# Sandwich layer on one core: first feed-forward norm on ScalarE and GpSimd, background products in quarters with rest steps, block 0's halves stored once

## The chip, the cores and the metric

The kernel runs on one core of one Trainium2 chip. The core has five engines with a queue of instructions each: TensorE (PE, matrix products; PEld is its weight load), VectorE (DVE), ScalarE (ACT), GpSimd (POOL) and SyncE (SP, which here only issues DMAs). Each engine works through its queue in order and waits on semaphores for the others. DMAs are issued from the queues of SP, ACT and POOL and run beside the engines. Products land in PSUM, eight banks of 512 float32 values on each of 128 partitions. The metric is the device time of one execution in microseconds; lower is better.

## What is computed

One transformer layer in float32 on 4096 tokens of 256 features:

```
x = x + layernorm(attention(layernorm(x)))
x = x + layernorm(ffn(layernorm(x)))

attention: q, k, v = x @ w_attn + b_attn, 16 heads of 16 features
           softmax(causal(q @ k.T / 4)) @ v, then @ w_proj + b_proj
ffn(x):    h = silu(x @ w1 * s1) * (x @ w2 * s2)        256 -> 1024
           h = gelu(h @ h1 * sh1); h = gelu(h @ h2 * sh2)  1024 -> 1024
           h @ w3 * s3                                  1024 -> 256
```

The feed-forward weights are drawn from -1, 0 and 1. The biases of attention are random.

## The kernel before, in words

The tokens are cut into 8 blocks of 512 (`NB`, `QB`), the 16 heads into 4 groups of 4 (`G`). An *item* (j, g) is query block j with head group g; there are 32 items, in order. Item (j, g) goes over the keys of blocks 0 to j in *steps* (`steps`, L876): 4j + 3 of them, with one or two units each, 8j + 5 *units* for the item and 1056 in all. A unit (`SharedUnit`, L828) is 1024 columns of scores for two heads in two PSUM banks: TensorE makes them (L843), VectorE takes their maximum (`mx`, L852), ScalarE the exponentials (`e_s`, L859), GpSimd clears what lies past the diagonal (L866), and three units later TensorE multiplies them with the values (`av`, L930). Three such pairs of banks go round (`ps_s`); one bank holds the `av` sums and one single bank (`ps_m`) is for everything else.

The score products take q and k in a rounded type (float32r). To keep the precision, q and k are split into a rounded upper half and the rest (`hi`, `lo`, in `features`, L519), and both halves are stored to DRAM twice, so that the 64 rows of a head's contraction hold all four pairs of halves. `load_rows` (L554) reads 128 such rows, two heads, in one DMA of 256 KB; `queries` (L566) and `keys` (L577) call it. The keys of the next item are asked for during the current one (`ask`, L585), for every item anew. All these loads go through SyncE's queue.

The rest of attention's work is *background*: generators that stop at marks and are run piece by piece between the steps. `prep(j)` (L599) loads block j, normalises it, transposes it (two groups of four 128x128 transposes), makes the k and q features (four products of two matmuls with 512 columns) and v. For blocks 0 and 1 its statistics and halves are VectorE's, later ScalarE's and GpSimd's. `project(j)` (L273) takes a finished block's weighed values through `w_proj`, its layer norm and the residual, and stores the sum in DRAM as `x1[j]`. Marks say what the next piece is: `PE` starts a product, `HALF` continues one, `ACT` is a pass of ScalarE, `BESIDE` is no stop here, `True` is anything else. A product and its continuation use the single bank `ps_m`, so an open product (`Background.open`) is finished before another begins.

After each step `Background.even(every)` (L95) runs at most one product piece, each `every` steps, and at most one ScalarE piece, likewise; other pieces run as they come. `every` is 1 for blocks 0 and 1, 2 for blocks 2 and 3, 3 from block 4 on (L1177). A piece is half a product: `prep` has 14 of them (two transposes, eight halves of features, four of v), `project` has 4. `finish` and the loop at L1138 run what is still missing when it is needed: q and k of block j + 1 at the start of item (j, 3), the whole prep at the start of block j.

Before the loop (L1115 to L1132) the kernel runs block 0's and block 1's norms, `biases` (L1102, which scales the q bias and makes the projection's share of the v bias, `pb`, from `wp`), block 0's features up to the first q, the loads of items 0 and 1, and the rest of block 0. Block 1's remaining prep then is background.

In the background also run `halve_weights` (L981, rounding the feed-forward weights on GpSimd) and, from item (7, 2) on, `norm_block(0, ...)` (L356) with `first_features` (L1060): the layer norm of `x1[0]` for the feed-forward, with statistics, scaling and lower halves on VectorE, and its eight transposes in one of the three score bank pairs. The result `xT0` is what the feed-forward begins with. `feed_forward` (L1249) then goes block by block through the four matrices on TensorE, and does the next block's norm (`norm_block` again) and the last block's `project` beside it.

Two flags computed on the device choose slower code for unusual data (`attention(False)`, `feed_forward(False, ...)`); they do not run here.

Of the kernel before, what the change touches and what calls it, by code (L numbers as in the profile page):

```python
# [17 lines left out]
P = 128  # L18
# [11 lines left out]
class Background:  # L30
# [6 lines left out]
    def __init__(self, beside=lambda: None):  # L37
        self.work = deque()
        self.beside = beside
        self.at = 0  # L40
        self.open = None

# [52 lines left out]
    def even(self, every):  # L95


        self.at += 1
        pe, act = not self.at % every, not (self.at + 1) % every
        for job in list(self.work):  # L100
            if job[3] in (self.PE, self.HALF):
                if pe and self.open in (None, job):
                    pe = False
                    self.run(job)
                    self.open = job if job[3] == self.HALF else None
            elif job[3] != self.ACT:
                self.run(job)
            elif act:
                act = False
                self.run(job)  # L110
# [7 lines left out]
def sandwich_kernel(  # L118
# [154 lines left out]
    def project(j, room):  # L273
# [35 lines left out]
        for half in range(0, NT, 2):  # L309
            ps = room.bank(f"py_{j}_{half}").rearrange("p (t f) -> p t f", t=2)  # L310
            for t in range(2):
                yield room.within(t)
                for c in range(DC):
                    nc.tensor.matmul(  # L314
                        ps[:, t, :],
                        lhsT=oT[:, c, (half + t) * P : (half + t + 1) * P],
                        rhs=wp[:, c, :],
                        start=(c == 0),
                        stop=(c == DC - 1),
                    )  # L320
# [83 lines left out]
    def attention(shared):  # L404
# [8 lines left out]
        with ExitStack() as actx:  # L413
# [22 lines left out]
            class Room:  # L436


                def within(self, n):
                    return Background.HALF if shared and n else Background.BESIDE  # L440
# [34 lines left out]
            def constants():  # L475
# [38 lines left out]
                (s, j): scratch.tile([H, 2, 2, HD, QB], F32, tag=f"{s}_{j}", name=f"{s}_{j}")  # L514
# [4 lines left out]
            def features(j, s, c, engine):  # L519
# [3 lines left out]
                for d in range(DC):  # L523
                    yield room.within(d)
                    nc.tensor.matmul(  # L525
                        ps,
                        lhsT=wqk[d][:, i * D + c * P : i * D + (c + 1) * P],
                        rhs=xTs[j][:, d, :],
# [16 lines left out]
                for half, part in enumerate((hi, lo)):  # L545
                    for d in range(2):
                        at = (d, half) if i else (half, d)
                        queue = nc.gpsimd if shared and j < 2 and half else nc.sync
                        queue.dma_start(
                            out=halves_of[s, j][8 * c : 8 * (c + 1), at[0], at[1]], in_=part  # L550
                        )
                stored.add((s, j, c))

            def load_rows(tag, name, key, j, h):  # L554

                t = (piece if key == "k" else query)(tag, name, F32R)
                nc.sync.dma_start(
                    out=t.bitcast(F32),
                    in_=halves_of[key, j][h : h + 2].rearrange("h a b d n -> (h a b d) n"),
                )  # L560
# [16 lines left out]
            def keys(n, c):  # L577

                for pr in range(2):
                    kT[n, c, pr] = load_rows(  # L580
                        f"k{asked[0] % RING}_{pr}", f"k{n}_{c}_{pr}", "k", c, 4 * (n % G) + 2 * pr
# [17 lines left out]
            def prep(j, engine=nc.gpsimd):  # L599
# [30 lines left out]
                for c in range(DC):  # L630
                    ps = room.bank(f"pt_{j}_{c}")
                    for t in range(NT):
                        nc.tensor.transpose(
# [11 lines left out]
                for half in range(0, NT, 2):  # L645
                    ps = room.bank(f"pv_{j}_{half}").rearrange("p (t f) -> p t f", t=2)
                    for t in range(2):
                        yield room.within(t)
                        for c in range(DC):
                            nc.tensor.matmul(  # L650
# [408 lines left out]

            def first_features(pts):  # L1060
# [41 lines left out]
            def biases():  # L1102
                nc.vector.tensor_scalar(bqk[:, 0:DC], bqk[:, 0:DC], SCALE, None, ALU.mult)
# [15 lines left out]
            biases()  # L1119
            while ("q", 0, 0) not in stored:  # L1120
                bg.piece(works[0])
            for n in range(2):
                queries(*items[n])
                keys(*chunks[n])
            while bg.piece(works[0]) is not False:
                pass
            if shared:
                bg.add(("prep", 1), works[1], PREP)
                bg.work[0][3] = Background.PE
            else:  # L1130
# [3 lines left out]
            for n, (j, g) in enumerate(items) if shared else ():  # L1134
# [14 lines left out]
                if (j, g) == (NB - 1, G - 2):  # L1149
                    for _ in halving:  # L1150
                        pass
                    bg.add(("norm", 0), norm_block(0, room, first_features), NORM)
# [3 lines left out]
                for p, (shapes, parts) in enumerate(steps(j)):  # L1156
# [19 lines left out]
                    if j < 2 or p < NT * j:  # L1176
                        bg.even(1 + j // 2 - j // 6)  # L1177
# [71 lines left out]
    def feed_forward(halves, xT0, W):  # L1249
# [6 lines left out]
        with ExitStack() as fctx:  # L1256
# [12 lines left out]
            class Room:  # L1269
                def within(self, n):  # L1270
                    return Background.BESIDE
# [236 lines left out]
```

## Time and profile before

| | |
|---|---|
| median of 3 runs | 2053.32 us (2049.6 to 2054.11) |
| the profiled execution's own time | 2048.42 us |
| its span, first to last instruction | 2046.5 us |
| mean granted TensorE clock | 0.986 |
| PE, DVE, ACT, POOL busy | 1825.3, 1609.8, 1399.2, 552.2 us |
| first score maximum | 39.8 us |
| blocks 0 to 3 of attention | 53.0, 75.1, 107.0, 147.8 us |
| blocks 4 to 7 | 185.7, 216.7, 253.8, 295.4 us |
| feed-forward | from 1378 us to the end |
| DMA | 202.09 MB, mean 99 GB/s |

Blocks are counted from their first score maximum to the next block's. A view by stretches gives, for each engine, how long it was busy and with how many instructions, and the clock that the throttle granted TensorE as a share of full speed. In a timeline a line is a group of equal instructions of one engine: its start, its duration, and in brackets how long the engine was idle before it and whose work ended that. "SPq" and "POOLq" are DMA issues. A wait is put down to what came last.

### The profile page before, as it was taken

The page shows a single profiled execution, that of the slowest core. Times are in us where ns is not written, and L with a number is a line of the kernel's source. Part 1 is how long each engine was busy: PE and PEld are TensorE (multiplying, and loading weights), DVE is VectorE, ACT ScalarE, POOL GpSimd, SP SyncE. Part 2 cuts the span into 40 slices and gives each one's busy share as a digit, 9 for nine tenths or more (in the row PEclk, how much of TensorE's full clock was granted, in tenths as well). Part 3 has the DMA queues.
Part 4 walks back from the last instruction along what each step waited for, and adds up shares of the span by engine and source line. Part 5 has one row for each costly group of instructions (what it writes and reads, how often), then busy time and mean ns, then how long its engine had stood idle before and what let it go on. Part 6 is the DMA issues. An engine that isn't in the chain of part 4 may idle for free.

```text
span 2046.5 us, 28401 instructions
## 1 busy us (share of the span) xinstructions
PE 1825.3 (89%) x10518; PEld 932.5 (46%) x10518; DVE 1609.8 (79%) x1894; ACT 1399.2 (68%) x1598; POOL 552.2 (27%) x871
## 2 busy tenths in 40 slices
PE   4799989988888888888888887889999999999997
PEld 2333332322322322223222222228888888888886
DVE  3689998998999999999999999985546456465453
ACT  2699999999999999999999998982212222222221
POOL 3264545434435335333333110000120000000000
PEclk8899999999999999999999998999999999999999
DMA  6756645444235333553234213103100000000000
GB/s 168 229 179 219 191 133 180 147 154 159 98 131 183 116 103 124 161 163 115 76 136 156 98 44 101 63 9 114 53 11 21 15 7 21 1 21 21 1 11 15
DMA packets 134909, 202.09 MB, mean 99 GB/s; under 512 B 16064, under 2 KB 60736, under 8 KB 134752
## 3 DMA queue, kind: packets, MB, share of 16 engines
q1 hardware_dynamic: 130496, 194.56, 29.3%
q0 software_dynamic: 2480, 4.35, 1.0%
q8 instruction: 87, 1.43, 0.3%
q10 hardware_dynamic: 1776, 1.18, 0.3%
q14 instruction: 70, 0.57, 0.1%
HBM read 137.91 MB, written 62.13 MB: 98 GB/s over the span
## 4 chain that ended last, share of the span: by engine, by line
PE 46%; ACT 21%; DVE 19%; issue 6%; DMA 4%; POOL 2%; SPq 1%; ACTq 0%; POOLq 0%; DVEq 0%
PE z L1358 21%; ACT e_s L859 19%; DVE mx L852 18%; PE av L930 7%; PE s L843 7%; PE za L1358 3%; PE zb L1358 2%; PE pyf L1440 2%; DMA k<-k 1%; PE py L314 1%; PE pk L525 1%; PE pv L650 1%; PE pq L525 1%; ACT junk L211 1%; DMA q<-hiq 0%
## 5 line engine op out<-in xcount | busy, mean ns | idle before, releaser
L852 DVE TENSOR_REDUCE mx<-s 128x1 f32<-128x1024 f32 x1056 | 1219.8, 1217 | 72.1 <-PE s L843 66.6
L859 ACT ACTIVATE e_s<-s,shift 128x1024 f32<-128x1024 f32 x1056 | 1153.6, 1117 | 104.9 <-DVE mx L852 81.9
L843 PE MATMUL s<-q,k 64*128 64x512 f32 (+3 forms) x2304 | 517.7, 468 | 161.2 <-ACT e_s L859 144.7
L930 PE MATMUL av<-e_s,v 128*32 128x512 f32 (+2 forms) x4576 | 572.8, 575 | 7.9 <-POOL e_s L866 5.7
L843 PEld LDWEIGHTS s<-q,k 64*128 64x128 f32 x2304 | 208.9, 185 | 752.9 <-ACT e_s L859 652.2
L1425 ACT ACTIVATE fb<-z,sh 128x512 f32<-128x512 f32 x128 | 88.1, 689 | 364.8 <-PE z L1358 340.2
L1358 PE MATMUL z<-hb_0l,h 128*128 128x512 f32 x512 | 199.5, 390 | 0.0
L1358 PE MATMUL z<-hb_0h,h 128*128 128x512 f32 x512 | 199.5, 390 | 0.0
L866 POOL TENSOR_SCALAR_AFFINE_SELECT e_s<-e_s 128x256 f32<-128x256 f32 (+1 forms) x224 | 94.7, 440 | 337.4 <-ACT e_s L859 337.4
L233 POOL TENSOR_TENSOR rstd<-ve,neghalf 128x4 f32<-128x4 f32 (+1 forms) x22 | 20.8, 944 | 608.8 <-DVE ve L231 603.0
L930 PEld LDWEIGHTS av<-e_s,v 128*32 128x32 f32 x4576 | 97.2, 109 | 151.5 <-issue 116.1
L1325 DVE CAST hb_1h<-fb 128x512 fp32r<-128x512 f32 x64 | 27.4, 428 | 155.7 <-ACT fb L1425 155.7
L1402 ACT ACTIVATE sl<-za,s 128x512 f32<-128x512 f32 x64 | 44.0, 690 | 120.4 <-PE za L1358 60.9
L1325 DVE CAST hb_0h<-fb 128x512 fp32r<-128x512 f32 x64 | 28.1, 440 | 99.6 <-ACT fb L1425 99.6
L1358 PEld LDWEIGHTS z<-hb_0h,h 128*128 128x128 f32 x512 | 96.1, 188 | 20.0
L1358 PEld LDWEIGHTS z<-hb_0l,h 128*128 128x128 f32 x512 | 96.2, 188 | 19.8
L1011 POOL TENSOR_SCALAR wc<-wc 128x256 f32<-128x256 f32 x88 | 75.8, 861 | 7.8
L1010 POOL TENSOR_TENSOR wc<-wc,wh 128x256 f32<-128x256 f32 x88 | 64.3, 730 | 7.2
L1012 POOL TENSOR_TENSOR fit<-fit,wc 128x256 f32<-128x256 f32 x88 | 64.2, 730 | 7.3
L1009 POOL CAST wh<-wc 128x256 fp32r<-128x256 f32 x88 | 35.0, 397 | 108.4 <-DMA wc<-in_h_t_dram 75.9
L1440 PE MATMUL pyf<-w,hb_1l 128*128 128x256 f32 x256 | 61.8, 284 | 0.0
L1440 PE MATMUL pyf<-w,hb_1h 128*128 128x256 f32 x256 | 61.7, 283 | 0.0
(257 smaller groups left out, 1970.3 us busy)
## 6 DMA issues: line engine op xcount, KB each, us to landing
k<-k SPq DMA_DIRECT2D x288, 256.0 KB
q<-q SPq DMA_DIRECT2D x64, 256.0 KB
x<-in_x_dram SPq DMA_DIRECT2D x16, 512.0 KB
k<-hik SPq DMA_DIRECT2D x32, 256.0 KB
q<-hiq SPq DMA_DIRECT2D x32, 256.0 KB
wc<-in_h_t_dram SPq DMA_DIRECT2D x64, 128.0 KB
r_h<-wh SPq DMA_DIRECT2D x64, 128.0 KB
h<-r_h SPq DMA_DIRECT2D x32, 256.0 KB
```

Of the source, the lines that this page charges most:

```text
L843: nc.tensor.matmul(self.both[:, i, col : col + n], lhsT=kT[G * j + g, c, pr][r, tt * P : (tt + 1) * P], rhs=qT[j, g][pr][r, QB - n :], sta ...
L852: nc.vector.tensor_reduce(next(columns), self.both.rearrange("p a n -> p (a n)"), AX.X, ALU.max)
L859: nc.scalar.activation(e, self.both, AF.Exp, bias=shifts[j])
L866: nc.gpsimd.affine_select(out=here, in_=here, compare_op=ALU.is_ge, fill=0.0, base=0, pattern=[[0, here.shape[1]], [1, P]], channel_multip ...
L930: nc.tensor.matmul(self.av[h * HW : (h + 1) * HW, QB - n :], lhsT=vb[kt // NT][:, kt % NT, o : o + HW], rhs=of(es, h), start=(kt == 0 or k ...
L1010: nc.gpsimd.tensor_tensor(w, w, hi, ALU.subtract)
L1011: nc.gpsimd.tensor_scalar(w, w, 0.0, None, ALU.is_equal)
L1012: nc.gpsimd.tensor_tensor(fit, fit, w, ALU.mult)
L1325: nc.vector.tensor_copy(hi, full)
L1358: nc.tensor.matmul(ps, lhsT=w[c], rhs=single(part[:, c, :]), start=(c == 0 and i == 0), stop=(c == kc - 1 and i == parts - 1),)
L1425: nc.scalar.activation(h, z, AF.Gelu, scale=sc[:, oc : oc + 1])
L1440: nc.tensor.matmul(ps[:, 0:D], lhsT=single(part[:, c, t * P : (t + 1) * P]), rhs=(w3_r if halves else w3_sb)[:, c, :], start=(c == 0 and i ...
```

## The change

Five things, in the order of the diff:

1. `Background.even` gets the number of product pieces for a step, the period of product steps, the period of ScalarE pieces, and a number of rest steps: with `rest`, the step that ends a product starts no other piece of TensorE or ScalarE, and product pieces pause until `rest` steps later. Blocks 0 to 2 run two pieces per product step (each step; each second step for block 2) with no rest; blocks 3 to 7 run one piece each step and rest 3. The ScalarE periods are 1, 1, 2, 2, 3, 3, 3, 2 for blocks 0 to 7.
2. Products are cut into quarters: features by half their columns and by the two matmuls, v and `py` by single matmuls, transposes into two and two. `prep` has 28 pieces, `project` 8.
3. Block 0's halves of q and k are stored once; its loads read the rows twice (`broadcast_to`), for k in two DMAs of 64 rows. The other blocks' copies lie in another order. Item 0's keys are loaded from GpSimd's queue.
4. Before the loop, `pb` is made after block 0's prep, and block 1's prep is run up to its first k feature.
5. Block 0's feed-forward norm is `norm_first`: sums and squares on ScalarE, scaling and both halves on GpSimd, transposes through the single bank in quarters. `project(6)` is finished before it is added.

```diff
-    def even(self, every):
+    def even(self, products, every, acts, rest):
         self.at += 1
-        pe, act = not self.at % every, not (self.at + 1) % every
+        pe = 0 if self.at % every or self.at < self.rested else products
+        act = self.at % acts == 1 % acts
         for job in list(self.work):
             if job[3] in (self.PE, self.HALF):
-                if pe and self.open in (None, job):
-                    pe = False
+                while pe and job[3] in (self.PE, self.HALF) and self.open in (None, job):
+                    pe -= 1
                     self.run(job)
                     self.open = job if job[3] == self.HALF else None
+                    if rest and not self.open:
+                        pe, act, self.rested = 0, False, self.at + rest
...
-                for d in range(DC):
-                    yield room.within(d)
+                cuts = 2 if shared else 1
+                for n, (cut, d) in enumerate(product(range(cuts), range(DC))):
+                    yield room.within(n)
+                    at = slice(cut * QB // cuts, (cut + 1) * QB // cuts)
                     nc.tensor.matmul(
-                        ps,
+                        ps[:, at],
                         lhsT=wqk[d][:, i * D + c * P : i * D + (c + 1) * P],
-                        rhs=xTs[j][:, d, :],
+                        rhs=xTs[j][:, d, at],
...
+                    queue = nc.gpsimd if shared and j < 2 and half else nc.sync
+                    kept = halves_of[s, j][8 * c : 8 * (c + 1)]
+                    for d in range(2) if j else ():
                         at = (d, half) if i else (half, d)
-                        queue = nc.gpsimd if shared and j < 2 and half else nc.sync
+                        queue.dma_start(out=kept[:, at[0], :, at[1]], in_=part)
+                    if not j:
+                        queue.dma_start(out=kept[:, :, half] if i else kept[:, half], in_=part)
...
+                elif key == "k":
+                    for i in range(2):
+                        rows = part[i : i + 1].rearrange("u d b n -> u (d b) n")
+                        queue.dma_start(
+                            out=to[i * P // 2 : (i + 1) * P // 2],
+                            in_=rows.broadcast_to([2, 2 * HD, QB]),
+                        )
+                else:
+                    rows = part.rearrange("h a (d u) n -> (h a d) u n", u=1)
+                    queue.dma_start(out=to, in_=rows.broadcast_to([P // 2, 2, QB]))
...
+            def norm_first():
+                xj = xb[0] = load_block(0, x1[0])
+                for _ in range(3):
+                    yield True
+                yield Background.ACT
+                mv = stat.tile([P, NT, 2], F32, tag="mv", name="mvf_0")
+                for t in range(NT):
+                    mean_of(xj[:, t, :], mv, t)
+                    yield Background.ACT
+                    spread_of(xj[:, t, :], mv, t)
+                    yield Background.ACT if t < NT - 1 else True
+                rstd = rstd_of(mv)
+                xh = room.tokens(0)
+                for t in range(NT):
+                    shift_and_scale(xh[:, t, :], xj[:, t, :], mv, rstd, t, nc.gpsimd)
+                    yield True
+                yield True
+                yield Background.PE
...
+                for c in range(DC):
+                    ps = room.bank(f"ptf_0_{c}")
+                    for t in range(NT):
+                        if t == NT // 2:
+                            yield Background.HALF
+                        nc.tensor.transpose(
+                            ps[:, t * P : (t + 1) * P], xh[:, t, c * P : (c + 1) * P], ident
+                        )
+                    nc.scalar.copy(xT[:, c, :], ps)
+                    hi, lo = (t[:, c, :] for t in xT0)
+                    nc.gpsimd.tensor_copy(hi, xT[:, c, :])
+                    nc.gpsimd.tensor_tensor(lo, xT[:, c, :], hi, ALU.subtract)
+                    yield Background.PE if c < DC - 1 else True
...
-            biases()
+            nc.vector.tensor_scalar(bqk[:, 0:DC], bqk[:, 0:DC], SCALE, None, ALU.mult)
             while ("q", 0, 0) not in stored:
                 bg.piece(works[0])
             for n in range(2):
                 queries(*items[n])
-                keys(*chunks[n])
+                keys(*chunks[n], nc.sync if n or not shared else nc.gpsimd)
             while bg.piece(works[0]) is not False:
                 pass
+            biases()
             if shared:
                 bg.add(("prep", 1), works[1], PREP)
                 bg.work[0][3] = Background.PE
+                while ("k", 1, 0) not in stored:
+                    bg.step()
...
-                    bg.add(("norm", 0), norm_block(0, room, first_features), NORM)
+                    bg.finish(("project", NB - 2))
+                    bg.add(("norm", 0), norm_first(), NORM)
...
-                        bg.even(1 + j // 2 - j // 6)
+                        bg.even(1 + (j < 3), 1 + (j == 2), (1, 1, 2, 2, 3, 3, 3, 2)[j], 3 * (j > 2))
```

## The prediction

> **What bounds the kernel now.** I read the engines' busy time by stage first (columns: stretch; PE, PEld, DVE, ACT and POOL busy with counts; granted clock; DMA share; GB/s). The stretches are block 0's attention, blocks 1, 5, 6 and 7, and the feed-forward stage; their bounds are the first score maxima (`mx`) of each block.
>
> ```profile
> core 0: us, PE busy (x) PEld busy (x) DVE busy (x) ACT busy (x) POOL busy (x), PEclk, DMA share, GB/s
> 39.00:92.00 53.00, 40.18 (x212) 17.36 (x212) 29.00 (x33) 29.73 (x40) 16.95 (x38) 0.77 0.72 221
> 92.00:168.00 76.00, 68.64 (x446) 25.93 (x446) 63.58 (x61) 67.21 (x90) 37.47 (x65) 1.00 0.62 206
> ...
> 608.00:825.00 217.00, 186.65 (x1202) 58.28 (x1200) 209.60 (x188) 206.34 (x227) 92.28 (x146) 1.00 0.41 133
> 825.00:1079.00 254.00, 218.78 (x1404) 68.27 (x1402) 246.36 (x222) 241.06 (x243) 95.07 (x147) 1.00 0.41 131
> 1079.00:1378.00 299.00, 248.35 (x1584) 73.47 (x1584) 289.62 (x282) 276.57 (x270) 39.39 (x66) 0.98 0.24 79
> 1378.00:2046.00 668.00, 653.38 (x3144) 551.03 (x3144) 349.81 (x707) 159.53 (x222) 52.76 (x61) 0.99 0.08 24
> ```
>
> The feed-forward's 668 us are TensorE's, in an order the change leaves alone. In late attention VectorE (97%) and ScalarE (95%) are both nearly full: back to back one `mx` takes 1.13 us (42 in 47.63 us on the chain). Block 0 is another thing: no engine is full, the clock is 0.77 and DMA moves 221 GB/s. Next the ramp, in order of time.
>
> ```profile
> 9.42 1.38 DVE L237 TENSOR_SCALAR x<-x,mv,rstd 128x256 f32<-128x256 f32 x4 [1.00 <-POOL rstd L233]
> 12.37 2.05 PE L1106 MATMUL pb<-wp,bv 128*128 128x256 f32 x4 [12.37 <-DMA wp<-in_w_proj_dram]
> 14.21 1.06 PE L633 MATMUL pt<-ident,x 128*128 128x128 f32 x4
> ...
> 23.24 2.60 SPq L549 DMA_DIRECT2D q<-hiq  x2
> ...
> 33.79 0.84 SPq L557 DMA_DIRECT2D q<-q  x2
> ...
> 38.98 0.80 PE L843 MATMUL s<-q,k 64*128 64x512 f32 x2 [5.88 <-DMA k<-k]
> ```
>
> Block 0's rows are normalised at 10.8, but their transposes wait in TensorE's queue behind `pb`, which waits for `wp`. The q halves' stores are issued at 23.24 and landed at 33.8; the first scores wait for the loads. TensorE's own windows show the price of that wait (PE busy, clock, DMA):
>
> ```profile
> 33.00:36.00 3.00, 0.09 (x1) 1.00 0.74 206
> 36.00:39.00 3.00, 0.03 (x2) 0.57 0.96 318
> 39.00:42.00 3.00, 1.57 (x4) 0.50 0.99 305
> ```
>
> The granted clock is 0.50 from 36.4 to 53.5, for most of the first item. Then the block norm of block 0 (item (7, 2)), on VectorE:
>
> ```profile
> 1232.29 0.42 DVE L196 BATCH_NORM_STATS2 bn<-x 128x6 f32<-128x256 f32 x1
> ...
> 1244.83 1.38 DVE L237 TENSOR_SCALAR y<-x,mvf,rstd 128x256 f32<-128x256 f32 x4 [1.14 <-POOL rstd L233]
> ...
> 1250.18 0.69 DVE L1067 TENSOR_TENSOR xT0l<-ptf,xT0h 128x512 fp32r<-128x512 f32 x1 [1.72 <-ACT xT0h L1066]
> ```
>
> Last, what a background product does in mid-attention (a half product of `project`, and the maximum after it):
>
> ```profile
> 706.75 1.13 PE L314 MATMUL py<-wp,oo 128*128 128x256 f32 x4
> ...
> 708.36 1.22 DVE L852 TENSOR_REDUCE mx<-s 128x1 f32<-128x1024 f32 x1 [0.20 <-PE s L843]
> ```
>
> **The change, part by part.** The sum goes against the profiled execution's 2048.42 us (span 2046.5); the median shown, 2053.32, lies 4.9 above it.
>
> *Ramp and block 0.* (a) `pb` goes behind block 0's v products. The transposes can end near 11.0 (last normalised slice at 10.8) instead of 15.3: 4.2 us earlier, and with them every feature; `pb`'s 2.05 us and VectorE's 0.42 us for `bp` come later, where TensorE stood idle (33 to 39). (b) Block 0's halves are stored once: 8 stores of 256 KB instead of 16. In 20.5 to 33.8 the first eight, 2 MB, landed; four should need about half of these 13.3 us, from 16.3 on: q loads at 23 to 26 instead of 33.8. (c) New work stands before the first scores on TensorE: v products end at 33.1 - 4.2 = 28.9, then `pb` 2.05, two transposes and copies 2 x (0.66 + 0.58), a k feature 2.0: 35.5. On VectorE, before the first `mx`, wait that feature's evacuation (0.69) and its halves (0.43 + 0.69): 37.4. Its `hi` buffer must first be stored by SyncE, behind 8 loads; the stores of c = 1 follow at about 30 and land by 36, just in time. First `mx` 37.4 instead of 39.8: 2.4 us. (d) TensorE now has work to 35.5, so I expect clock 1.00 in the first item; its 10.3 us of products in a 13.7 us item would be 5.2: about 10 us. Eight of block 1's 28 quarters are done before the loop, its last ones end in step (0, 3, 0), not in a flush at (1, 0), and the stalls at 66 to 80 shrink with 2 MB less to store: items 11.6, 15.2 and 12.5 become about 11, 11 and 10. Block 1 starts near 80 instead of 92.8: **-13 us**. Bounds: -2.4 (only the first `mx` moves) and -29 (20 units at 1.3 us).
>
> Against it: each block-0 key load becomes two issues of 128 KB with the rows read twice, two loads a pair, 64 more in all (0.43 us each on SyncE's queue, 288 before). After block 0 they are asked for an item ahead, 16 us or more; I take 0. The first item's four go to GpSimd's queue (0.60 us an issue), behind k's and q's lower halves; nothing waits behind them but the c = 1 stores. The before trace lands two 256 KB loads 5.7 us after issue, so four half loads from 23 land by 32, under the cover of (c); without that cover they cost up to 4.
>
> [...]
>
> [...]
>
> *Blocks 1 and 2.* Two quarters each step (block 2: each second step) are the old half at the old pace: 0, give or take 2.
>
> *Quarters, blocks 3 to 7.* Before: 14 pieces for each of 4 preps and 4 for each project, 78 in all from block 3. The price: items of block 6 take 65.1, 64.7, 63.5 and 60.5 us for the same 53 maxima, with 8, 8, 2 and 0 pieces. Block 5: 55.9, 54.5, 54.3, 52.0 with 7, 6, 1, 0. The items with 1 or 2 pieces are 2 to 3 us above the empty ones, which is ScalarE's part; the rest is 0.25 to 0.35 us a piece, 78 x 0.3 = 23 us. Why a quarter should cost less: a step holds scores 0.5 + values 1.06 + scores 0.5, some overlapped, 1.85 us of TensorE, against 2.27 of VectorE. A half, 1.13, overruns by 0.7, a quarter by 0.13. Four in a row overrun by 0.5, then two steps of rest give 0.8 back. I take 60%: **-14 us**. Bounds: -23 (all of it), and +23 (each quarter as dear as a half), since no row shows a lone quarter; the nearest, four matmuls of 256 columns for v, take the 2.0 us per eight that four of 512 take for k, so size alone adds nothing. One loss: block 3's pace falls from 4 steps a feature to 6, and at (3, 3) four quarters of prep 4 are still missing and issued at once: **+1.5**.
>
> *First norm.* Between 1232.3 and 1260.1 VectorE does 16 maxima, 18.1 us of 27.8: it loses 9.7, of it 5.5 in its own norm work, the rest waiting for `rstd`, `xT0h`, and scores at clock 0.50 (1248.2 to 1258.4). New: 8 ScalarE passes with their accumulator reads, about 0.6 each, 5 us in an item where ScalarE is busy 69 of 79 us; GpSimd's 4 x 0.55 and halves, where it is 5% busy; four short TensorE pieces in the single spare bank instead of a third of the score ring. **-8 us**, between -3 (ScalarE becomes the later one) and -9.7.
>
> Sum: -13 - 14 + 1.5 - 8 = -33.5, so 2015 for the profiled execution and, 4.9 above, **2020** against the median.
>
> **Rivals.** (A) *The ramp gives only its first 2.4 us*, since transfers set block 0's pace: for, 274 GB/s at 0.91 DMA share in 80.3 to 92.8; against, 2 MB less to store. 2020 + 10.6 = 2031. (B) *Quarters give nothing*: the same TensorE work in six steps, and ScalarE, at 95%, sets the pace: for, ScalarE's part in the item times; 2034. (C) *Slower*: a quarter issued in four consecutive steps delays four score pairs instead of two. If each costs p, 156 of them cost 156p against the 23 us removed, and the other parts bring 19.5: slower from p = 0.27 us, nearly the whole price of a half. At p = 0.4, 2053 + 62 - 23 - 19.5 = 2073. For it: a ring of three score buffers with little slack; against: 0.13 us overrun. (D) *The clock stays at 0.50 in the first item*, and the norm gains 3: 2020 + 4 + 5 = 2029.
>
> **How the numbers follow.** The forecast (2003 to 2030) 0.53, A 0.12, B 0.14, C 0.13, D 0.08. Low end: ramp -20, quarters -23, norm -9.7 give 2002; 1998 with room. High end: A and B together are 2045, and a small C reaches 2050. Within 0.2% (2049.2 to 2057.4), about what this kernel's measurement can tell from no change, only a C near its break-even falls: 0.04; slower the rest of C, 0.09; faster 0.87.
>
> **What would show it.** `pt` near 10 us and the first score maximum near 37; clock 1.00 through the first item; block 1 starting near 80; items (6, 0) and (6, 1) near 62; item (7, 2) near 72 with no 0.50 stretch; feed-forward unchanged at 668. Wrong if block 1 starts after 88, if items of blocks 3 to 6 are longer than before, or if TensorE waits for `k` loads after block 1.

## The result

The change made the kernel slower: 2100.07 us (2097.9 to 2101.25) against 2053.72 us for the kernel before beside it, a ratio of 1.0227 [1.0209, 1.0245]. The profiled execution took 2099.69 us with a span of 2097.8, 51.3 above the span before. The forecast was 2020. From the page of the changed kernel: its shares of the chain that ended last, the maxima (with the idle time ahead of them at the end), and block 0's key loads.

```profile
HBM read 137.91 MB, written 60.03 MB: 94 GB/s over the span
...
PE 48%; ACT 23%; DVE 12%; DMA 7%; issue 5%; SPq 2%; POOL 2%; ACTq 0%; POOLq 0%; DVEq 0%
...
L886 DVE TENSOR_REDUCE mx<-s 128x1 f32<-128x1024 f32 x1056 | 1220.4, 1215 | 108.4 <-PE s L877 92.1
...
k<-k SPq DMA_DIRECT2D x124, 128.0 KB
```

DMA is 7% of the chain, where it was 4%, although 2 MB less were written; the maxima wait 92 us for scores instead of 67. Block by block, from one block's first score maximum to the next block's (us):

| | first `mx` | block 0 | 1 | 2 | 3 | 4 | 5 | 6 | 7 |
|---|---|---|---|---|---|---|---|---|---|
| before | 39.8 | 53.0 | 75.1 | 107.0 | 147.8 | 185.7 | 216.7 | 253.8 | 295.4 |
| after | 50.8 | 63.2 | 97.9 | 122.1 | 144.8 | 180.0 | 226.0 | 249.5 | 291.5 |
| difference | +11.0 | +10.2 | +22.8 | +15.1 | -3.0 | -5.7 | +9.3 | -4.3 | -3.9 |

Up to the end of block 2 the kernel loses 59 us; afterwards it gains 7.6 in attention, and the feed-forward is unchanged at 672. Stretches of the changed kernel by blocks 0, 1, 2, 6, 7 and the feed-forward (busy time of PE, PEld, DVE, ACT, POOL, then granted clock, DMA share, GB/s):

```profile
core 0: us, PE busy (x) PEld busy (x) DVE busy (x) ACT busy (x) POOL busy (x), PEclk, DMA share, GB/s
50.80:114.00 63.20, 39.77 (x210) 19.72 (x210) 28.05 (x32) 25.94 (x31) 15.35 (x33) 0.69 0.48 143
114.00:212.00 98.00, 75.78 (x454) 30.33 (x454) 63.66 (x62) 70.14 (x95) 39.70 (x70) 0.89 0.47 149
212.00:334.00 122.00, 102.98 (x642) 37.63 (x642) 99.79 (x92) 100.50 (x126) 49.40 (x78) 0.92 0.50 163
...
885.00:1134.00 249.00, 218.75 (x1394) 66.67 (x1394) 244.41 (x220) 239.28 (x241) 97.80 (x152) 1.00 0.40 128
1134.00:1426.00 292.00, 245.21 (x1564) 71.53 (x1562) 284.11 (x261) 276.42 (x286) 44.34 (x74) 0.99 0.26 81
1426.00:2097.00 671.00, 656.33 (x3170) 551.97 (x3166) 352.13 (x713) 160.79 (x223) 54.28 (x64) 0.99 0.08 24
```

In block 0 DMA moves 143 GB/s at a share of 0.48, where before it moved 221 at 0.72. So the engines wait for transfers, and the transfers run slower than they did. Two stretches in which VectorE and ScalarE are mostly idle show how slow:

```profile
46.00:50.00 4.00, 0.00 (x0) 0.00 (x0) 0.24 (x1) 0.00 (x0) 0.00 (x0) 0.50 0.12 47
99.00:107.00 8.00, 3.58 (x15) 1.27 (x19) 2.42 (x2) 1.11 (x1) 0.41 (x1) 0.50 0.14 51
```

Something is under way that keeps 0.14 of 16 engines busy, 2.2 of them, and moves 51 GB/s. The changed kernel's timeline of the ramp names it:

```profile
9.52 1.44 PE L665 MATMUL pt<-ident,x 128*128 128x128 f32 x4 [9.52 <-DVE x L241]
...
13.43 3.78 PE L540 MATMUL pk<-xT,wqk 128*128 128x256 f32 x8 [0.68 <-ACT xT L669]
...
22.98 0.75 SPq L567 DMA_DIRECT2D q<-hiq  x1
...
24.62 2.72 POOL L579 DMA_DIRECT2D k<-k  x4
...
33.47 4.39 SPq L579 DMA_DIRECT2D k<-k  x4
...
37.96 2.41 SPq L567 DMA_DIRECT2D k<-hik  x1
38.14 0.74 PE L877 MATMUL s<-q,k 64*128 64x512 f32 x4
...
49.76 0.43 DVE L557 CAST hik<-fullk 128x512 fp32r<-128x512 f32 x1 [15.59 <-DMA k<-hik]
...
50.83 2.35 DVE L886 TENSOR_REDUCE mx<-s 128x1 f32<-128x1024 f32 x2
```

The transposes start at 9.5, the first scores at 38.1. But the first maximum stands in VectorE's queue behind a cast, whose buffer is free only when the upper half of k, c = 1, is stored. SyncE issues that store at 37.96, behind item 1's four key loads (L579), and it lands at 49.7: 11.7 us for 256 KB. The waits of the changed kernel (total, how many, the longest):

```profile
POOL wh L1043 <- DMA wc<-in_h_t_dram: 151.5, 25, 17.1
...
PE s L877 <- DMA k<-k: 26.1, 13, 3.5
...
PEld s L877 <- DMA k<-k: 21.4, 8, 3.5
...
DVE hik L557 <- DMA k<-hik: 15.6, 1, 15.6
```

TensorE waits 26 us for keys (10.7 before), and even for weight loads, which have nothing to do with attention, GpSimd waits twice as long (151.5 us against 75.9).

### The profile page after: what moved, and what is told of

It is laid out like the page before. It is cut to its first block, busy times and chain, and to the rows that moved or that the text cites. A ratio compares the mean times of both kernels' runs of the same rounds, so it can differ in the third digit from the quotient of the medians.

```text
span 2097.8 us, 28695 instructions
## 1 busy us (share of the span) xinstructions
PE 1864.7 (89%) x10646; PEld 958.2 (46%) x10646; DVE 1605.6 (77%) x1879; ACT 1400.3 (67%) x1614; POOL 560.7 (27%) x880
## 4 chain that ended last, share of the span: by engine, by line
PE 48%; ACT 23%; DVE 12%; DMA 7%; issue 5%; SPq 2%; POOL 2%; ACTq 0%; POOLq 0%; DVEq 0%
PE z L1432 22%; ACT e_s L893 22%; DVE mx L886 11%; PE av L964 8%; PE s L877 6%; PE pyf L1514 3%; PE za L1432 2%; PE zb L1432 2%; DMA k<-k 2%; DMA k<-hik 1%; PE py L320 1%; DMA avd<-av_sb 1%; SPq L579 1%; PE pk L540 1%; PE pv L684 1%
## 5 line engine op out<-in xcount | busy, mean ns | idle before, releaser
L877 PE MATMUL s<-q,k 64*128 64x512 f32 (+3 forms) x2304 | 536.9, 475 | 169.2 <-ACT e_s L893 130.1
L964 PEld LDWEIGHTS av<-e_s,v 128*32 128x32 f32 x4576 | 97.8, 110 | 151.5 <-issue 120.9
L1043 POOL CAST wh<-wc 128x256 fp32r<-128x256 f32 x88 | 35.0, 398 | 224.4 <-DMA wc<-in_h_t_dram 151.5
L1045 POOL TENSOR_SCALAR wc<-wc 128x256 f32<-128x256 f32 x88 | 75.9, 863 | 7.9
```

What stands on the lines that cost most here:

```text
L877: nc.tensor.matmul(self.both[:, i, col : col + n], lhsT=kT[G * j + g, c, pr][r, tt * P : (tt + 1) * P], rhs=qT[j, g][pr][r, QB - n :], sta ...
L964: nc.tensor.matmul(self.av[h * HW : (h + 1) * HW, QB - n :], lhsT=vb[kt // NT][:, kt % NT, o : o + HW], rhs=of(es, h), start=(kt == 0 or k ...
L1045: nc.gpsimd.tensor_scalar(w, w, 0.0, None, ALU.is_equal)
```

## The experiments

The first theory was that block 0's key loads are narrow: the source of each, `rows.broadcast_to([2, 2 * HD, QB])`, has the repetition of 2 as its outermost dimension, and such a load keeps about two of the 16 DMA engines busy, an estimate from the 0.14 of 16 in 99 to 107 us. Rivals: the order of the stores in SyncE's queue alone; the number and small size of the loads; the reading of rows twice; the quarters.

**e1: block 0's halves stored twice, as before, and everything else of the change.**

```diff
-                if j:
-                    queue.dma_start(out=to, in_=part.rearrange("h a d b n -> (h a d b) n"))
-                elif key == "k":
...
+                queue.dma_start(out=to, in_=part.rearrange("h a d b n -> (h a d b) n"))
```

> The changed kernel with block 0's halves stored twice again and read by one DMA of 128 rows per load; all else as changed. Theory 1 (the 64-row loads that read their rows twice run on few of the 16 DMA engines: in 99 to 107 us of the changed kernel 2.2 were active on average, at 52 GB/s, while TensorE waited for k): the first maximum moves from 50.8 to about 41, blocks 0 to 2 take about 50, 75 and 107 us instead of 63.2, 97.9 and 122.1, and the time is about 2045. Theory 2 (quarters and rest steps disturb the score ring): blocks 0 to 2 stay near 63, 98 and 122 and the time at 2085 or more.

Measured 2033.0 us, 0.9913 [0.9896, 0.9929]; blocks 0 to 2 take 47.6, 76.1 and 106.0. The loss of the change is in part 3, in the single stores and their loads; the rest gains 18 us.

**e2: the changed kernel, each key load of block 0 as four DMAs of 32 rows without repetition.**

```diff
-                    for i in range(2):
-                        rows = part[i : i + 1].rearrange("u d b n -> u (d b) n")
+                    for i in range(4):
                         queue.dma_start(
-                            out=to[i * P // 2 : (i + 1) * P // 2],
-                            in_=rows.broadcast_to([2, 2 * HD, QB]),
+                            out=to[i * P // 4 : (i + 1) * P // 4],
+                            in_=part[i // 2].rearrange("d b n -> (d b) n"),
```

> The changed kernel with block 0's halves still stored once, but each key load of block 0 cut into four DMAs of 32 rows that read no row twice: double the issues, a quarter of the size. Theory 1 (few DMA engines for the source that is read twice): 32 rows spread over all engines, blocks 0 to 2 come back to about 50, 78 and 110, time about 2050. Theory 3 (the number of DMA issues is what costs): 124 issues more at some 0.5 us each on SyncE, blocks 0 to 2 longer than in the changed kernel, time 2110 to 2140.

Measured 2034.84 us, 0.9918 [0.9902, 0.9935]: 65 us less than the changed kernel by the form of these loads alone, with the halves still stored once and twice as many DMAs. Blocks 0 to 2 take 49.9, 76.2 and 105.7.

**e3: the changed kernel, with the rest of block 0's prep, and so its stores, ahead of item 1's loads.**

```diff
             for n in range(2):
                 queries(*items[n])
                 keys(*chunks[n], nc.sync if n or not shared else nc.gpsimd)
-            while bg.piece(works[0]) is not False:
-                pass
+                while bg.piece(works[0]) is not False:
+                    pass
```

> The changed kernel with the loads of item 1 issued after the rest of block 0's prep, so that SyncE issues the c = 1 stores of k and q ahead of these six loads. It tells what the wait of VectorE for that store (15.6 us idle before the first maximum) is worth by itself. If the order of the stores is the cause of the late first maximum: it moves from 50.8 to about 40 and the time to about 2090, with blocks 0 to 2 as long as in the changed kernel. If the slow loads alone are the cause: the first maximum stays near 50 and the time at 2100.

Measured 2089.98 us, 1.0188 [1.0171, 1.0205]. The first maximum moves from 50.8 to 38.0, but blocks 0 to 2 take 65.1, 97.0 and 125.0. The blocked cast is a true part of the loss, and the smaller one: 12.8 us at the first maximum, 10 us in all.

**e4: the kernel before, with part 3 alone** (halves of block 0 stored once, loads of 64 rows twice read, item 0's keys from GpSimd).

```diff
+                elif key == "k":
+                    for i in range(2):
+                        rows = part[i : i + 1].rearrange("u d b n -> u (d b) n")
+                        queue.dma_start(
+                            out=to[i * P // 2 : (i + 1) * P // 2],
+                            in_=rows.broadcast_to([2, 2 * HD, QB]),
+                        )
```

> The kernel before with one part of the change alone: block 0's halves stored once, read by two 64-row DMAs per key load, item 0's keys on GpSimd's queue. Theory 1: blocks 0 to 2 lengthen as in the changed kernel, by 10, 23 and 15 us, time 2090 to 2105. Theory 2 (quarters): no longer than before, time about 2050, or shorter by the 2 MB less to store.

Measured 2133.71 us, 1.0398 [1.0379, 1.0416]: 82 us from part 3 alone, more than the whole change loses and above the range of either theory. Blocks 0 to 2 take 69.9, 102.4 and 125.7.

**e5: e1 with the old pace** (product steps each 1, 2 or 3 steps, two quarters each, no rest).

```diff
-                        bg.even(1 + (j < 3), 1 + (j == 2), (1, 1, 2, 2, 3, 3, 3, 2)[j], 3 * (j > 2))
+                        bg.even(2, 1 + j // 2 - j // 6, 1 + j // 2 - j // 6, 0)
```

> e1_stored_twice with the background at the old pace: both quarters of a half in one step, every 1, 1, 2, 2, 3, 3, 3, 3 steps for blocks 0 to 7, ScalarE pieces likewise, no rest. It tells what quarters and rest steps are worth from block 3 on. If they help as e1's blocks 3 to 6 suggest (797.2 us against 804.0 before): 803 to 806 us for these blocks and about 2040. If they are worth the 12 us of the prediction: about 2046. If they are worth nothing, and e1's gain came from elsewhere: 2033.

Measured 2048.61 us, 0.9981 [0.997, 0.9992], 15.6 above e1. Blocks 3 to 6 take 816.0 us in all, 797.2 in e1 and 804.0 before: quarters with rest gain, and the old pace in the new frame is worse than it was in the old one.

**e6: the kernel before with the new first norm alone.**

```diff
-                    bg.add(("norm", 0), norm_block(0, room, first_features), NORM)
+                    bg.finish(("project", NB - 2))
+                    bg.add(("norm", 0), norm_first(), NORM)
```

> The kernel before with the first norm alone on ScalarE and GpSimd, its transposes through the single bank. If that is where block 7 gained in e1 (285.6 us instead of 295.4): block 7 takes 286 to 288 and the time is 8 us shorter, about 2044. If a first ScalarE pass that waits for its rows holds up the exponentials behind it (3.8 us in the changed kernel, where long key loads stood ahead of it on SyncE's queue): 4 us less gain, about 2048.

Measured 2042.54 us, 0.9951 [0.9936, 0.9967]. Block 7 takes 287.2 instead of 295.4, -8.2; item (7, 2) 70.5 instead of 79.2.

**e8: e1 with the stores first, as in e3.**

```diff
-            while bg.piece(works[0]) is not False:
-                pass
+                while bg.piece(works[0]) is not False:
+                    pass
```

> e1_stored_twice with the loads of item 1 issued after the rest of block 0's prep, as in e3. If the order of stores ahead of loads is worth by itself what e3 showed (first maximum 12.8 us earlier): first maximum near 37 instead of 45.8, block 1 starts near 84 instead of 93.5, time about 2024. If block 0 is paced by transfers, whatever their order: block 1 starts near 92 and the time stays at 2032.

Measured 2032.29 us, 0.9899 [0.9877, 0.9921]: the first maximum moves only from 45.8 to 45.2, and block 1 starts at 94.1. The cast still waits 9.4 us for its store (11.3 in e1), although that store now stands ahead of item 1's loads.

**e9: e8 with block 0's k stored once and read twice in one DMA of 128 rows,** the repetition inside, so that 64 rows are outermost.

```diff
+                if key == "k" and not j:
+                    rows = part.rearrange("h d (b u) n -> (h d b) u n", u=1)
+                    queue.dma_start(out=to, in_=rows.broadcast_to([P // 2, 2, QB]))
+                else:
+                    queue.dma_start(out=to, in_=part.rearrange("h d a b n -> (h d a b) n"))
```

> e8 with block 0's keys stored once and still read twice, but in one DMA of 128 rows whose outer dimension is 64 rows and whose inner one is the repeat (the rows of the contraction stand in another order; q of block 0 is stored twice). If the narrow outer dimension of 2 was the cost and not the repeated reading: as fast as e8 or some us faster for the 1 MB less to store, 2018 to 2026. If reading the same rows twice is the cost: slower than e8 by 30 us or more.

Measured **2016.21 us, 0.9822 [0.9801, 0.9842]**, a little below its range, 84 us below the changed kernel and 16 below e8. Reading rows twice is not the cost. The 16 us can't be put down to k's single store alone, for e9 to e12 differ from e8 in one thing more: they keep q and the other blocks' halves as `[H, HD, 2, 2, QB]`, so that the 128 rows of each store lie at one even stride in DRAM. In e8, as in e1, e2, e14 and the kernel before, these rows lie as 8 heads of 16 rows. The stores from GpSimd's queue (number, size, median us from issue to landing), in e8:

```profile
k<-lok POOLq DMA_DIRECT2D x8, 256.0 KB, 7.2
q<-loq POOLq DMA_DIRECT2D x8, 256.0 KB, 9.0
```

and in e9:

```profile
q<-loq POOLq DMA_DIRECT2D x8, 256.0 KB, 5.0
k<-lok POOLq DMA_DIRECT2D x6, 256.0 KB, 3.4
```

In the ramp, where nothing else is under way, block 0's k stores in the changed kernel, which have the even stride, bring DMA's share to 1.00 (21.0 to 21.5 us); those of e8 reach 0.67 at most (19.5 to 22.5 us, in steps of 0.5). No run changes the stores' form alone, so what it is worth stays open. The four items of block 0 in e9:

```profile
39.90:52.10 12.20, 9.61 (x46) 5.72 (x50) 7.34 (x10) 4.92 (x5) 4.14 (x10) 0.72 0.32 115
52.10:63.70 11.60, 9.73 (x80) 4.96 (x68) 7.93 (x10) 8.31 (x9) 5.09 (x11) 1.00 0.80 266
63.70:74.20 10.50, 6.28 (x43) 3.48 (x42) 6.38 (x10) 6.72 (x9) 4.07 (x9) 0.92 0.98 322
74.20:82.80 8.60, 8.05 (x52) 3.49 (x52) 5.69 (x5) 5.90 (x8) 1.58 (x4) 0.70 0.48 171
```

DMA reaches 322 GB/s at a share of 0.98, and block 1 starts at 82.8 (114.0 in the changed kernel, 92.8 before).

**e10: e9 with each key load as two DMAs of 64 rows again,** the same number and size as in the changed kernel.

```diff
-                    rows = part.rearrange("h d (b u) n -> (h d b) u n", u=1)
-                    queue.dma_start(out=to, in_=rows.broadcast_to([P // 2, 2, QB]))
+                    for i in range(2):
+                        rows = part[i].rearrange("d (b u) n -> (d b) u n", u=1)
+                        queue.dma_start(
+                            out=to[i * P // 2 : (i + 1) * P // 2],
+                            in_=rows.broadcast_to([2 * HD, 2, QB]),
+                        )
```

> The kernel with one wide load (2016) but with each key load of block 0 as two DMAs of 64 rows and 128 KB again, as in the changed kernel; only the source's order differs from the changed kernel's: 32 rows outermost and the repeat inside, instead of the repeat of 2 outermost. Theory (the outermost 2 of the source narrows the load to about two engines): no loss, 2016 to 2025, and the keys' transfers overlap as the others do. Rival (the number or the small size of the loads, or reading rows twice, costs): 2035 or more, towards 2090.

Measured 2018.61 us, 0.9839 [0.9823, 0.9856]. Neither 124 loads of 128 KB nor reading rows twice costs what the changed kernel loses. The key loads of block 0 by source line, first the changed kernel (issue times in ns; the landing is that of the four from GpSimd):

```profile
L579 SPq DMA_DIRECT2D k<-k x124: 474/514/4030, 33.5 to 1277.7; - x124
...
DMA to landing us min/median/max: 6.5/7.4/8.5
```

and e10:

```profile
L578 SPq DMA_DIRECT2D k<-k x124: 507/594/1242, 32.7 to 1202.7; - x124
...
DMA to landing us min/median/max: 3.5/3.8/4.0
```

The same bytes to the same 64 partitions land in 3.8 us instead of 7.4, and no issue holds SyncE for more than 1.2 us, where it was 4.0.

**e11: e9 with `pb` ahead of block 0's transposes, as before the change.**

```diff
+            biases()
...
             while bg.piece(works[0]) is not False:
                 pass
-            biases()
```

> The kernel with one wide load (2016) but with the biases' product pb ahead of block 0's transposes again, as before the change. Theory (what the transposes gained by going first was given back, since the features then ran at half clock): 2016 plus or minus 3, the first features at about 2 us instead of 3.8 and started 4 us later, the first maximum near 39.9. Rival (the earlier start is worth its 4.2 us): 2020 or more, the first maximum near 44.

Measured 2019.57 us, 0.9849 [0.9833, 0.9866]. The time lies between the two expectations and can't be told from e10's 2018.61. The first maximum says more: 43.9, as the rival had it. Timeline of e11:

```profile
12.16 2.04 PE L1170 MATMUL pb<-wp,bv 128*128 128x256 f32 x4 [12.16 <-DMA wp<-in_w_proj_dram]
...
17.52 3.74 PE L540 MATMUL pk<-xT,wqk 128*128 128x256 f32 x8 [0.68 <-ACT xT L663]
22.04 1.99 PE L540 MATMUL pq<-xT,wqk 128*128 128x256 f32 x8 [0.78 <-ACT fullk L549]
...
38.48 3.50 PE L540 MATMUL pk<-xT,wqk 128*128 128x256 f32 x8 [0.68 <-ACT xT L663]
...
43.86 2.35 DVE L880 TENSOR_REDUCE mx<-s 128x1 f32<-128x1024 f32 x2
```

and of e9:

```profile
13.34 3.78 PE L540 MATMUL pk<-xT,wqk 128*128 128x256 f32 x8 [0.68 <-ACT xT L663]
...
17.90 3.68 PE L540 MATMUL pq<-xT,wqk 128*128 128x256 f32 x8 [0.78 <-ACT fullk L549]
...
36.02 2.00 PE L540 MATMUL pk<-xT,wqk 128*128 128x256 f32 x8 [0.67 <-ACT xT L663]
...
39.89 2.35 DVE L880 TENSOR_REDUCE mx<-s 128x1 f32<-128x1024 f32 x2
```

My reading had been that the earlier start is worth nothing, since the first products then run slowly (3.78 us where the same take 1.99; the granted clock in 12 to 20 us of e9 reads 1.00, not half). That falls in part. With `pb` ahead the first product is slow as well (3.74), but the second takes 1.99 where e9's takes 3.68, so that of the transposes' 4.2 us the third product keeps 2.5 (it starts at 24.81 instead of 22.35). The rest of the 4.0 us at the first maximum comes from the k feature at 38.48: it runs 3.50 us, at a granted clock of 0.54 to 0.61, where e9's takes 2.00 at 1.00. Block 1 starts only 1.1 us later in e11 (83.9).

**e12: e9 with the k of all blocks stored once.**

```diff
-                if key == "k" and not j:
+                if key == "k":
```

> The kernel with one wide load (2016) with the halves of k stored once in all blocks, and every key load reading them twice within one DMA, 64 rows outermost. Theory (a twice-read source with many outermost rows costs nothing): 2010 to 2018, some 15 MB less written than with two stores. Rival (repeated reading costs where many loads do it): each load slower, 2025 or more.

Measured 2016.24 us, 0.9828 [0.9811, 0.9844]. The written bytes fall from 61.08 to 53.74 MB and the time stays: reading rows twice is no cost, and fewer stores in late attention are no gain that can be seen beside an interval of some 3 us to either side. (The expectation's 15 MB was too many; the runs show 7.3.)

**e13 and e14: the outer dimension without any repetition.** So far the repetition and the 2 had always gone together. Both kernels load block 0's keys in four DMAs of 32 rows, none read twice in a DMA. In e13 the source is two interleaved sets of 16 rows, in e14 the rows are stored so that 32 follow one another.

```diff
-                            in_=part[n // 2].rearrange("d b n -> b d n"),
+                            in_=part[n // 2].rearrange("b d n -> (b d) n"),
```

> The kernel with two 64-row loads (2018.6), but each key load of block 0 is four DMAs of 32 rows, no row is read twice within a DMA, and the rows of a head are put in the order half, feature instead of feature, half. In the source as stored this is an outer dimension of 2 (the halves) over 16 rows that don't follow one another; bytes, number of DMAs and destination are those of the run with the merged source. Theory (an outermost 2 narrows the load to about two engines, repeated or not): the loss is back, 2070 to 2110, and TensorE waits for key loads at about 50 GB/s. Rival (reading rows twice within a DMA is what was slow): as with the merged source, 2016 to 2025.

> The same as the run with the split source, with block 0's keys stored half by half, so that the 32 rows that each DMA reads follow one another and the source has one outer dimension of 32. Both theories: 2016 to 2025, as with two 64-row loads. If this one is slow as well, the number of loads is the cause, and neither theory holds.

Measured 2090.99 us, 1.0184 [1.0167, 1.0201], for e13 and 2034.25 us, 0.9907 [0.9891, 0.9924], for e14. The loads of e13, 64 KB each:

```profile
L577 SPq DMA_DIRECT2D k<-k x248: 575/576/4470, 37.1 to 1275.3; - x124
...
  PE s L874: 27.9, 14
...
DMA to landing us min/median/max: 4.7/7.7/9.1
```

and of e14:

```profile
L577 SPq DMA_DIRECT2D k<-k x248: 302/419/2276, 38.8 to 1217.8; - x124
...
  PE s L874: 8.2, 3
...
DMA to landing us min/median/max: 2.6/3.3/4.2
```

57 us, as many DMAs of the same size, not a row read twice: the outermost 2 is the cause. (That the 16 rows of e13 don't follow one another is not: in the changed kernel, with the same 2 outermost, the 32 rows do, and it is as slow.) TensorE's waits (27.9 us) and the rate while they last (53 GB/s at a share of 0.15, 99 to 107 us) are those of the changed kernel. e14 also missed its range and lies 16 us above e10, as e2 does. Both differ from e10 in two things: four loads of 32 rows instead of two of 64, and stores in 8 heads of 16 rows instead of at an even stride. e1 and e8, with the same kind of stores and one load of 128 rows, take 2033.0 and 2032.3, hardly less than e14. That speaks for the stores and against a price of the loads' number or size, but no run separates the two.

## Why the prediction was wrong

**The step that failed** is "After block 0 they are asked for an item ahead, 16 us or more; I take 0", with "four half loads from 23 land by 32" under it. I costed the loads by their bytes and number, by the row in which two 256-KB loads land 5.7 us after issue, and did not ask whether the source's form changes how fast they land (128 KB in 7.4 us in the changed kernel, 3.8 in e10). The form of these loads alone costs **65 us** in the changed kernel (against e2) and 57 in e13 (against e14); part 3 as a whole costs 82 by itself (e4). It enters in four ways, each in the traces of the changed kernel. It slows the keys themselves (26 us of TensorE's waits, 7.8 in e2). It holds SyncE up to 4.0 us an issue, and with it all that is queued behind. It delays the store for which VectorE's cast waits (15.6 us). And the granted clock is lower, a mean of 0.69 in block 0 (0.79 in e2). "An item ahead" was no cover: of an item's keys in blocks 0, 1 and 2, such loads bring all, a half and a third.

How such a load is spread over the engines, no run shows: the share of 0.14 in the changed kernel and of 0.15 in e13, 2.2 and 2.4 of 16, is a mean over 8 us with whatever else was under way, and which engines they were can't be read from it. What e13 shows is that the outermost 2 is slow without any repetition (7.7 us to landing, 3.3 in e14).

**The other steps** can be read where that fault is away. e2 is the change with nothing but these loads replaced, four of 32 rows for two of 64 (span 2031.6, 14.9 below before). e9 has, besides, the stores ahead of item 1's loads, q's halves of block 0 stored twice, and stores at an even stride (span 2016.0, 30.5 below before; the blocks of e10 and e12 are within 2 us of it).

| term | predicted | e2 | e9 | from |
|---|---|---|---|---|
| ramp and block 0 | -13 | -0.8 | -10.0 | block 1 starts at 92.0 and 82.8 instead of 92.8 |
| blocks 1 and 2 | 0 ± 2 | -0.2 | -0.5 | 181.9 and 181.6 instead of 182.1 |
| quarters, blocks 3 to 7 | -12.5 | -7.7 | -12.0 | blocks 3 to 6 -6.2 and -10.4, block 7 -1.5 and -1.6 beyond the norm |
| first norm | -8 | -8.2 | -8.2 | e6 |
| key loads of block 0 | 0 | +65 in the changed kernel | | 2100.07 - 2034.84 |

(The feed-forward is 2 us longer in e2.) So a second step failed: even without the slow loads the change takes 2035, not 2020. Its ramp gives almost nothing, near rival A (2031), and no more in e1, with one load of 128 rows (block 1 starts at 93.5). Its quarters give three fifths of their term. That e9 comes out near the forecast is luck: half of its gain comes with things that the change does not have.

(a): `pt` at 9.5, right. (c): the new work on TensorE ends at 38.2, not at 35.5, mostly because the first two products took 3.78 us each, where the kernel before has 1.99; that gives back 3.6 of the 4.2 us of (a). The first maximum at 37.4 would also have needed the c = 1 store "by 36, just in time", and it was issued only at 37.96. In e3, with that store ahead, the maximum is at 38.0. (b): right in direction; the first q loads are issued at 30.68 in the changed kernel, and at 28.4 in e9, against 33.79 before, not at 23. (d): wrong. The clock of the first item is 0.72 in e2 and e9 and 0.63 in the changed kernel, not 1.00, which is in part rival D's condition, and the item takes 12.2 us or more. That work up to 35.5 would bring the full clock was my estimate from the windows at 33 to 42 us; in e9 TensorE is busy for 4.65 of the 6 us from 31 to 37, at 1.00, and the first item still runs at 0.72, so what sets the clock there was not shown. What the ramp gave in e9 came from the last two items, 10.5 and 8.6 instead of 15.2 and 12.5, where the transfers had held TensorE. In e2 these two take 17.8 and 8.2.

*Quarters.* Blocks 3, 4 and 6 gain 3.0, 5.4 and 4.4 in e9, block 5 loses 2.4 (5.1 in e2). The price of a half was read too high: from items (6, 0) and (6, 1) to (6, 2), and from (5, 0) and (5, 1) to (5, 2), the prediction's rows give 0.04 to 0.27 us a piece, where it takes 0.25 to 0.35. The +1.5 at (3, 3) is not to be seen (34.5 us, 35.2 before). Items (6, 0) and (6, 1) take 64.2 and 62.3; only the second is "near 62". Rival C, slower quarters, falls with e5: against the old pace the quarters with rest gain 15.6 us. That they gain by the smaller overrun that was costed, no run shows.

*Norm.* Item (7, 2) is 70.4 in e9, but 76.3 in the changed kernel, where ScalarE's first pass stands waiting. Timeline of the changed kernel:

```profile
1278.26 2.50 SPq L168 DMA_DIRECT2D x<-x  x1
...
1281.98 16.83 SPq L575 DMA_DIRECT2D k<-k  x14
1293.93 0.42 ACT L207 ACTIVATE junk<-x 128x256 f32<-128x256 f32 x1 [3.82 <-DMA x<-x]
```

and of e9:

```profile
1201.00 0.59 SPq L168 DMA_DIRECT2D x<-x  x1
...
1204.99 8.84 SPq L579 DMA_DIRECT2D k<-k  x14
```

`x1[0]`, asked for 15 us ahead, is still not there, and the same 14 ordinary key loads take 16.8 us to issue instead of 8.8 (9.3 in e2). ScalarE was the safe place for the norm in my costing, and it is; what makes its passes late is the load that they stand behind. Block 5 has the same: a pass waits 5.0 us for `x` of the last prep, and the block takes 226.0 instead of 221.8 in e2 and 219.1 in e9. That these two waits come from the narrow loads is read from e2 and e9, where neither is there.

Of the signs set down beforehand, "block 1 starts after 88" and "TensorE waits for `k` loads after block 1" came true, and longer items in blocks 3 to 6 did for block 5 (item (5, 1) 61.5 us instead of 54.5). The rivals named other things, and no case held a transfer that gets slower: the range ended at 2050 with no room for the key loads, which stood in the sum at 0 with a bound of 4.

## What to carry to other kernels

Read a DMA's access pattern as well as its bytes: here, with an outermost 2 in the source, all of DMA moved 51 to 53 GB/s at a share of 0.14 to 0.15 while TensorE waited, and the kernel lost 57 to 65 us; the same repetition inside cost nothing that could be seen (2018.61 us in e10). A saving of stores that changes the form of the loads is to be costed at the loads, and at everything queued behind them: the issuing engine's queue, the buffers that wait for a store, and the engine whose next instruction writes such a buffer (VectorE, 15.6 us). When a large change loses time, undo it part by part before judging any part: here the norm was worth what had been forecast, the quarters three fifths of it and the ramp next to nothing, and the form of one load turned the sum round. And when an experiment gives data another layout, look at every DMA that reads or writes it: e9's gain over e8 came with a new form of the stores, too.

## What the runs showed that I had not expected

- Where such loads hold TensorE up, all of DMA together moves 53 GB/s with a source split 2 x 16 rows (e13), and 51 with a 2 that is a repetition, 2.2 to 2.4 of 16 engines; four loads of the same bytes in one piece (e14) land in 3.3 us instead of 7.7.
- 124 such loads of 128 KB, 16 of 200 MB, slow others down: weight loads that have nothing to do with them keep GpSimd waiting 144.2 us in e13 and 80.4 in e14 (151.5 in the changed kernel, 77.9 in e2), and near 1282 us issues of ordinary loads on SyncE take almost twice as long (16.8 us for 14, 9.3 in e2).
- 256-KB stores whose rows lie at an even stride land in 3.4 to 5.0 us (e9), those in 8 heads of 16 rows in 7.2 to 9.0 (e8), and the kernel before, with the slower form, has 6.8 and 8.9.
- Reading each row twice in one DMA cost nothing that could be seen where the rows are outermost (2016.21 us in e9, 2016.24 in e12), and 7.3 MB less written in the later blocks gained nothing.
- The first products ran at half speed while the clock column reads 1.00: in e11 a feature takes 3.74 us at 17.5 and 1.99 at 22.0, with 1.00 shown in 17 to 20. In the kernel before, the same product at 17.28 took 1.99 after the same `pb` and transposes. The second product, too, takes 3.68 us in e9 and 3.78 in the changed kernel, and 1.99 in e1 and e14 after the same first ones. What ends this slow start earlier stays open.
